# Summing two halves of a norm product ahead of a matmul with ones, and taking the norm's inverse root on ScalarE

## The chip, the cores and the metric

The kernel runs on one core of a Trainium2 chip. Times are device microseconds of that core; a run's time is compared by the median of several executions. A separate execution, taken by the hardware profiler, gives the profile.

## What is computed

Two cross-attention layers follow each other on x (16 batches, 256 query tokens, 320 channels, 20 heads of 16), with a context of 256 tokens of 512 channels per batch. The change touches the second layer only. Cut to what matters, with 252 text tokens and 4 image tokens:

```python
probs_t = softmax(q @ k_t.T * scale)                 # per head, 256 x 252
text_out = probs_t @ v_t
qsem = probs_t @ text_ehs                            # per head, 256 x 512
qsem = qsem / max(norm(qsem), 1e-12)
ip_n = ip_ehs / max(norm(ip_ehs), 1e-12)
fused = q @ k_ip.T * scale + 0.5 * (qsem @ ip_n.T)
probs_ip = softmax(fused) * spatial_mask
out = (text_out + probs_ip @ v_ip) @ W_out + b_out + residual
```

The long vectors qsem are never formed. Their squared norm is p' G p, where p is a row of probabilities and G the 252 x 252 matrix of products of the text tokens (the Gram matrix).

## The kernel before

Work is cut into slots: a slot is one group of four heads of one batch, five slots to a batch, 80 slots for the first layer and 80 for the second. `slot1(k)` writes out the order of TensorE's work in a slot of the second layer by hand; between its parts `fill` steps through background tasks (projections, keys, values, the image softmax, the output of the batch before), each of which has a list of due times. Only TensorE's order is pinned in the slots. The order on VectorE (DVE in the profile), ScalarE (ACT), GpSimd (POOL) and the DMA-issuing SyncE (SP) is made by a scheduler, from the order in which operations are recorded and its own picture of their times.

A slot k of the second layer goes like this:

- `both1(k, t)`, for the two halves t of the text keys: transposed scores for slot k in the two PSUM banks "T" (L775), scores for slot k + 2 in "S" (L780) with their row maxima on VectorE (L781, tile `mn`), and the exponential on ScalarE (L786) into P, which has a tile for each of the two pairs of heads u, [128, 2 halves, 2 heads, 256].
- `rounded1(k, u)`: ScalarE writes a rounded half of P into R (L804, tile `ctb`), and GpSimd the rest P - R into W (L805, tile `wt`), each a 128x512 operation per half t.
- `norm1(k, u, n)`, one slot later: for each half n of the keys, four or three matmuls multiply the Gram blocks `gm` with R (L814), and VectorE multiplies the result by W, in place (L815). Each result takes one of the three PSUM banks "X", which rotate among these products, the background's matmuls and the transposed maxima (L792).
- `attend1(k)`, two slots later, at the start of a slot: eight matmuls gather the values (L823), and eight more with the matrix `zone` (L826), whose one column of ones adds W up over the keys of both halves n, into the same PSUM tile "P".
- `settle1` transposes the tile (L870), and divides (L873, L874). The norm goes into `nt`, column 5.

After a batch's last group, `image_softmax` works on all five groups at once, 128x40 values: u = max(norm, a tiny multiple of the squared row sum) (L889 on GpSimd, L891 on VectorE), then its inverse root r as the power -1/2 on GpSimd (L894), the fused scores a (L897, L899), their maximum m4 (L902), the exponential (L906), its sum and the reciprocal (L909, L910), and the products with the mask (L912, L914). VectorE transposes the outcome (L921), `close1` multiplies it with the image values (L931), adds it to the gathered heads (L932), splits the sum into two parts (`split`, tile `ho`: L511 on ScalarE, L512 and L513 on VectorE) and projects it (L522). `image1` (L500) and the projection of the next query tokens (`hq`) are other background work that the prediction speaks of. In the last batch the image softmax runs twice, for four groups and for the last one.

The power's exponent is a tile of -0.5, `w1["mhalf"]`, which `weights3` puts into a corner of a buffer.

Of the kernel before, what the change touches and what calls it, by code (L numbers as in the profile page):

```python
# [10 lines left out]
AF = mybir.ActivationFunctionType  # L11
ALU = mybir.AluOpType
# [4 lines left out]
B = 16  # L17
S = 256
# [3 lines left out]
CP = 384  # L22
# [8 lines left out]
NG = H // 4  # L31
# [10 lines left out]
def RAMP(t):  # L42
    return t if t < -5 or t > 3 else (t + 5) * 0.375
# [5 lines left out]
def xattn2(  # L49
# [27 lines left out]
    nc = tc.nc  # L77
    f = lambda ap: ap.bitcast(F32)
    mm = nc.tensor.matmul

    def dma(out, in_):
        nc.sync.dma_start(*(f(ap) if ap.dtype == FR else ap for ap in (out, in_)))
# [6 lines left out]
    def bank(tag="X"):  # L89
        return ps.tile([128, 512], F32, tag=tag, name=tag, bufs=BANKS[tag])  # L90
# [8 lines left out]
    def buf(tag, shape, dtype=F32, bufs=1, name=None):  # L99
        if tag in ("wB", "wD", "vr", "raw"):  # L100
            return sb.tile(shape, dtype, tag=tag, name=name or tag, bufs=bufs)
        size = 1
        for d in shape[1:]:
            size *= d
        if tag not in slots:
            slots[tag] = [0, dtype] + [const_tile([128, max(size, words.get(tag, 0))], f"{tag}_{i}", dtype) for i in range(bufs)]
        n, kind, *ring = slots[tag]
        assert kind == dtype and len(ring) == bufs, tag
        slots[tag][0] += 1
        t = ring[n % bufs][: shape[0], :size]  # L110
        names = "abcd"[: len(shape) - 1]
        if len(names) > 1:
            t = t.rearrange(f"p ({' '.join(names)}) -> p {' '.join(names)}", **dict(zip(names, shape[1:])))
        return t

    def const_tile(shape, tag, dtype=F32):
        return const.tile(shape, dtype, tag=tag, name=tag)
# [162 lines left out]
    zone = const_tile([128, 32], "zone")  # L280
# [82 lines left out]
    w1, v1t, gmt = {}, [], []  # L363
# [70 lines left out]
    def weights3():  # L434
        gm = buf("vr", [128, 3 * (H * V0W + 16)], FR, bufs=3, name="gm")
        gm = gm[:, : 7 * 128].rearrange("p (g n) -> p g n", n=128)
        nc.gpsimd.memset(f(gm), 0.0)
        gmt.append(gm)
        yield
        if len(gmt) == 2:  # L440
            one, two = [buf("rs", [128, 2 * S], bufs=2, name="one") for i in range(2)]
            w1["vb"], w1["mhalf"] = one[:, :CP], one[:, CP : CP + NG * 8]
            w1["pT"], w1["pip"] = two[:, :S], two[:, S:].rearrange("p (f c) -> p f c", c=32)
            nc.vector.memset(w1["mhalf"], -0.5)
            nc.gpsimd.memset(w1["pip"], 0.0)

    ct1 = {}
# [158 lines left out]
    QK, P, W, R = {}, {}, {}, {}  # L606
# [202 lines left out]
    def norm1(k, u, n):  # L809

        gm = get("t1", k // NG - B)[1]
        yp = bank().rearrange("p (h t) -> p h t", h=2)
        for i, (gb, kt) in enumerate(blocks[n]):
            mm(yp, gm[:, gb], R[k, u][:, kt], start=i == 0, stop=i == len(blocks[n]) - 1)  # L814
        nc.vector.tensor_mul(W[k, u][:, n], yp, W[k, u][:, n])  # L815

    def attend1(k):
        b, g = divmod(k - NS, NG)
        v, pv = get("t1", b)[0], bank("P")
        for n in range(2):  # L820
            for s in range(4):
                h = V1W * (4 * g + s)
                mm(pv[32 * s : 32 * s + 32, :S], v[:, n, h : h + 32], P[k, s % 2][:, n, s // 2], start=n == 0, stop=False)  # L823
        for n in range(2):
            for s in range(4):
                mm(pv[32 * s : 32 * s + 32, :S], zone, W[k, s % 2][:, n, s // 2], start=False, stop=n == 1)  # L826
        settle1(b, g, pv)

    def slot1(k):
# [30 lines left out]
    def settle1(b, g, pv):  # L860
        hn = hsn
        if g == 0:
            norms[b] = buf("tmp", [128, NG, 8, 6], bufs=2, name="n1")
        nt = norms[b]
        if "na" not in w1:
            w1["na"], masks = [buf("nt", [128, 2, 8, 32], bufs=2, name="na") for i in range(2)]
            w1["bmask"] = masks.rearrange("p a f c -> p (a f c)")[:, :CP]
            dma(w1["bmask"], bmask_d)
        na = w1["na"][:, (NG * b + g) % 2]
        nc.vector.transpose(na.rearrange("p f c -> p (f c)"), pv[:, :S])  # L870
        nc.gpsimd.tensor_copy(nt[:, g], na[:, :, 16:22])
        rz = pv[:, S : S + 8]
        nc.vector.reciprocal(rz, na[:, :, 16])  # L873
        nc.vector.tensor_mul(  # L874
            hn[:, g // 2, :, g % 2], na[:, :, 0:16], rz.unsqueeze(2).to_broadcast([128, 8, 16])
        )
        if g == NG - 1:
            nc.gpsimd.tensor_copy(hn[:, 2, :, 1], hn[:, 2, :, 0])
            later(0.4, lambda: gather(1, b))

    def image_softmax(b, lo=0, hi=NG):

        gs, n = slice(lo, hi), hi - lo
        nt, si = norms[b][:, gs], get("o1", b)[1]
        pool = nc.gpsimd
        small = lambda n, t: buf(t, [128, NG, 8] + ([n] if n > 1 else []))[:, gs]

        u = small(1, "u")
        pool.tensor_mul(u, nt[:, :, :, 0], nt[:, :, :, 0])  # L889
        yield  # L890
        nc.vector.scalar_tensor_tensor(u, u, EPS2 / 4, nt[:, :, :, 5], op0=ALU.mult, op1=ALU.max)  # L891
        yield
        r = small(1, "r")
        pool.tensor_tensor(r, u, w1["mhalf"].rearrange("p (f s) -> p f s", f=NG)[:, gs], op=ALU.pow)  # L894
        b4 = lambda t: t.unsqueeze(3).to_broadcast([128, n, 8, NIP])
        a = small(NIP, "a")
        pool.tensor_mul(a, nt[:, :, :, 1:5], b4(r))  # L897
        by_group = lambda t: t[:, :, : NG * NIP].rearrange("p f (g n) -> p g f n", n=NIP)[:, gs]
        pool.tensor_add(a, a, by_group(si))  # L899
        yield  # L900
        m4 = small(1, "m4")
        nc.vector.tensor_reduce(m4, a, axis=AX.X, op=ALU.max)  # L902
        yield
        pool.tensor_sub(a, a, b4(m4))
        yield
        nc.scalar.activation(a, a, AF.Exp, scale=SCALE)  # L906
        yield
        z4 = small(1, "z4")
        nc.vector.tensor_reduce(z4, a, axis=AX.X, op=ALU.add)  # L909
        nc.vector.reciprocal(z4, z4)  # L910
        yield
        pool.tensor_mul(z4, z4, mk.unsqueeze(1).to_broadcast([128, n, 8]))  # L912
        pi = w1["pip"]
        pool.tensor_mul(by_group(pi), a, b4(z4))  # L914
        if hi < NG:
            return
        vb = w1["vb"]
        dma(vb, vipd[NIP * b : NIP * (b + 1)].unsqueeze(0).to_broadcast([32, NIP, CP]))
        yield
        pT = w1["pT"]  # L920
        nc.vector.transpose(pT, pi.rearrange("p f c -> p (f c)"))  # L921
        nc.vector.tensor_mul(vb, vb, w1["bmask"])
        return pT, vb
# [38 lines left out]
    def task(key, times, make, *needs):  # L962
        tasks[key] = [times, 0, make, needs, len(tasks)]
# [14 lines left out]
    def get(*key):  # L978
        while key not in results:
            step(key)  # L980
        return results[key]
# [20 lines left out]
    def shifted(n, *times):  # L1002

        return [RAMP(n + t) for t in times]
# [10 lines left out]
    for c in range(B // 2):  # L1015
        n, k = 10 * c, [("k0", c)] if c else []
# [11 lines left out]
    for b in range(B):  # L1028
        n = NS + 5 * b
        task(("k1", b), shifted(n, -7, -6.67, -6.33, -5.67, -5, -4.67), lambda b=b: keys1(b), ("w2",), *([("t1", b - 1)] if b else []), *([("w4", 1)] if b > 2 else []))  # L1030
        task(("t1", b), shifted(n, -3.67, -3, -2.67, -2.33), lambda b=b: tokens1(b), ("k1", b), ("w3", b % 2))
        task(("o1", b), shifted(n, -7.67, -7, -6.67, -5.33, -4.33, -4), lambda b=b: open1(b), ("w7",), ("c0", b), *([("o1", b - 1)] if b else []))
        task(("i1", b), shifted(n, 6.67, 6.67, 6.67, 7.33, 7.33, 7.67, 7.67, 8, 8.33), lambda b=b: image_softmax(b, NG - 1 if b == B - 1 else 0), ("gathered", 1, b), ("taken", B + b - 1), *([("i1a",)] if b == B - 1 else []))
        task(("c1", b), shifted(n + (1.67 if b > B - 3 else 0), 8.67, 8.67, 8.67, 8.67, 9, 9.67, 11.67, 13), lambda b=b: close1(b), ("i1", b), ("w4", 1))
    task(("i1a",), [2 * NS + 0.1], lambda: image_softmax(B - 1, 0, NG - 1), ("i1", B - 2))
    spread = lambda t, d, n: [t + d * i for i in range(n)]
    thirds = lambda n, t: [t + i // 3 + (0.2, 0.6, 1.0)[i % 3] for i in range(n)]
# [4 lines left out]
    for i in range(2):  # L1042
        task(("w3", i), [NS - 4 + 5 * i], weights3)
# [147 lines left out]
```

## Time and profile before

| | |
|---|---|
| median of 3 runs | 1643.64 us (1639.58 to 1647.11) |
| profiled execution, time | 1646.73 us |
| profiled execution, span from the first to the last instruction | 1644.9 us |
| busy: TensorE, its weight load | 94%, 75% |
| busy: VectorE, ScalarE, GpSimd | 73%, 50%, 72% |
| mean granted TensorE clock | 0.972 |
| second layer, one batch | about 55.1 us |

Busy shares are averages over the whole span; the two layers differ, so a stage is read by itself. A line such as L815 is a line of the kernel before. In a group's row stand the line, the engine, the operation, what it writes and reads, sizes, and the number of instructions; then the busy time in us and the mean of one in ns; then the idle time of that engine just ahead of them, and what ended it. A matmul of full-width floats appears as two records.

### The profile page before, as it was taken

The page shows a single profiled execution, that of the slowest core. Times are in us where ns is not written, and L with a number is a line of the kernel's source. Part 1 is how long each engine was busy: PE and PEld are TensorE (multiplying, and loading weights), DVE is VectorE, ACT ScalarE, POOL GpSimd, SP SyncE. Part 2 cuts the span into 40 slices and gives each one's busy share as a digit, 9 for nine tenths or more (in the row PEclk, how much of TensorE's full clock was granted, in tenths as well). Part 3 has the DMA queues.
Part 4 walks back from the last instruction along what each step waited for, and adds up shares of the span by engine and source line. Part 5 has one row for each costly group of instructions (what it writes and reads, how often), then busy time and mean ns, then how long its engine had stood idle before and what let it go on. Part 6 is the DMA issues. An engine that isn't in the chain of part 4 may idle for free.

```text
span 1644.9 us, 36268 instructions
## 1 busy us (share of the span) xinstructions
PE 1539.0 (94%) x13306; PEld 1239.6 (75%) x13306; DVE 1197.1 (73%) x2404; ACT 830.3 (50%) x1797; POOL 1184.0 (72%) x1131
## 2 busy tenths in 40 slices
PE   7789999999999899689999999999999999999996
PEld 6677878787878787577777777777777777777765
DVE  5467777677666677867777787778777887787685
ACT  5335445445454545435555455545555555555462
POOL 3358787868686867767687767767776787678675
PEclk9799999999999999789999999999999999999998
DMA  7766777777777676565324333343334233423301
GB/s 220 203 207 197 219 202 218 202 210 196 207 198 222 180 213 172 162 198 179 121 86 132 119 104 108 124 127 97 115 118 133 88 123 110 142 82 106 109 26 44
DMA packets 247742, 247.49 MB, mean 150 GB/s; under 512 B 31050, under 2 KB 231468, under 8 KB 247564
## 3 DMA queue, kind: packets, MB, share of 16 engines
q1 hardware_dynamic: 245356, 243.87, 50.1%
q8 instruction: 106, 1.74, 0.5%
q10 hardware_dynamic: 2208, 1.30, 0.3%
q14 instruction: 72, 0.59, 0.1%
HBM read 121.21 MB, written 88.18 MB: 127 GB/s over the span
## 4 chain that ended last, share of the span: by engine, by line
PE 54%; DVE 14%; DMA 10%; POOL 9%; ACT 5%; issue 4%; SPq 2%; ACTq 0%; POOLq 0%; DVEq 0%
PE X L205 16%; PE X L814 10%; PE X L522 7%; PE P L709 5%; POOL wt L805 4%; PE S L649 3%; PE P L823 3%; PE T L673 3%; DMA qs<-qd 3%; PE P L826 3%; PE T L775 2%; DMA qs<-mt 2%; DVE ho L512 2%; DMA kd<-kst 2%; DVE wt L815 2%
## 5 line engine op out<-in xcount | busy, mean ns | idle before, releaser
L679 POOL TENSOR_TENSOR P<-P,rs 128x512 f32<-128x512 f32 x320 | 412.6, 1310 | 171.3 <-ACT P L676 170.9
L805 POOL TENSOR_TENSOR wt<-P,ctb 128x512 f32<-128x512 f32 x320 | 422.4, 1335 | 117.1 <-ACT ctb L804 115.9
L814 PE MATMUL X<-ctb,gm 128*128 128x512 f32 x1120 | 328.8, 412 | 2.5 <-DVE wt L815 2.5
L676 ACT ACTIVATE P<-T 128x512 f32<-128x512 f32 x320 | 176.2, 595 | 234.5 <-PE T L673 118.4
L786 ACT ACTIVATE P<-T 128x512 f32<-128x512 f32 x320 | 174.1, 597 | 142.4 <-PE T L775 121.8
L815 DVE TENSOR_TENSOR wt<-X,wt 128x512 f32<-128x512 f32 x320 | 216.7, 679 | 25.7 <-PE X L814 23.0
L804 ACT ACTIVATE ctb<-P 128x512 fp32r<-128x512 f32 x320 | 195.8, 631 | 74.9 <-PE X L814 63.2
L814 PEld LDWEIGHTS X<-ctb,gm 128*128 128x128 f32 x1120 | 188.8, 188 | 49.4 <-DVE wt L815 5.2
L781 DVE TENSOR_REDUCE mn<-S 128x4 fp32r<-128x1008 f32 x160 | 191.1, 1194 | 0.6 <-PE S L780 0.6
L651 DVE TENSOR_REDUCE mn<-S 128x4 fp32r<-128x716 f32 x160 | 142.6, 891 | 0.0
L673 PE MATMUL T<-qs,ks 127*128 127x256 f32 x640 | 112.6, 296 | 22.9 <-DVE tmp L726 9.8
L649 PE MATMUL S<-ks,qs 125*128 125x256 f32 x640 | 119.1, 310 | 11.2 <-DVE mn L651 3.5
L709 PE MATMUL P<-P,vr 128*32 128x256 f32 x1920 | 128.9, 404 | 0.0
L649 PEld LDWEIGHTS S<-ks,qs 125*128 125x128 f32 x640 | 89.9, 197 | 48.3 <-issue 38.3
L522 PE MATMUL X<-ho,wF 128*128 128x256 f32 x768 | 112.9, 290 | 7.1 <-DVE ho L512 3.0
L894 POOL TENSOR_TENSOR r<-u,rs 128x40 f32<-128x40 f32 (+2 forms) x17 | 108.7, 6393 | 14.8 <-DVE u L891 14.7
L522 PE MATMUL X<-hq,wE 128*128 128x256 f32 x768 | 110.7, 288 | 6.6 <-POOL hq L512 3.1
L673 PEld LDWEIGHTS T<-qs,ks 127*128 127x128 f32 x640 | 93.3, 199 | 28.0 <-DVE tmp L726 11.7
L522 PEld LDWEIGHTS X<-ho,wF 128*128 128x128 f32 x768 | 103.6, 195 | 12.8 <-DVE ho L512 4.7
L522 PEld LDWEIGHTS X<-hq,wE 128*128 128x128 f32 x768 | 102.9, 194 | 11.0 <-POOL hq L512 3.8
L205 PE MATMUL X<-cta,wA 128*128 128x252 f32 (+1 forms) x720 | 100.9, 287 | 7.7 <-ACT wA L147 5.8
L650 DVE TENSOR_REDUCE mn<-S 128x4 fp32r<-128x308 f32 x160 | 74.8, 468 | 44.8 <-PE S L649 44.2
(196 smaller groups left out, 2814.9 us busy)
## 6 DMA issues: line engine op xcount, KB each, us to landing
qd<-q SPq DMA_DIRECT2D x96, 384.0 KB
qs<-tph SPq DMA_DIRECT2D x64, 308.0 KB
kd<-kst SPq DMA_DIRECT2D x73, 256.0 KB
rawc<-in_cT_dram SPq DMA_DIRECT2D x60, 256.0 KB
qs<-qd SPq DMA_DIRECT2D x80, 192.0 KB
ks<-kd SPq DMA_DIRECT2D x80, 192.0 KB
ks<-kd SPq DMA_DIRECT2D x160, 96.0 KB
qs<-qd SPq DMA_DIRECT2D x160, 96.0 KB
```

Of the source, the lines that this page charges most:

```text
L205: last = mm(out, lhs(a, k), rhs(b, k), start=i == 0, stop=i == len(terms) - 1)
L522: mm(pp, w(s, k, slice(m * 128, (m + 1) * 128)), a[:, t], start=i == 0, stop=i == len(terms) - 1)
L649: mm(sp[:, h], Q[: XROW + T0, h, t * 128 : (t + 1) * 128], K[: XROW + T0, h], start=True, stop=True)
L673: mm(st[p][:, j], K[:KS0, 2 * p + j, t * 128 : (t + 1) * 128], Q[:KS0, 2 * p + j], start=True, stop=True)
L676: exp = anchor(nc.scalar.activation(pt, st[p], AF.Exp, scale=SCALE))
L679: anchor(nc.gpsimd.tensor_mul(pt, pt, rs[:, t : t + 1].to_broadcast([128, 2, S])))
L709: mm(pv[32 * s : 32 * s + 32, o : o + S], v[:, vt, h : h + 32], P[k, s // 2][:, t, s % 2], start=vt < 2, stop=vt != 1,)
L781: anchor(nc.vector.tensor_reduce(maxes[k + 2][:, t], sp[:, :, :T1], axis=AX.X, op=ALU.max))
L804: nc.scalar.activation(R[k, u][:, t], P[k, u][:, t], AF.Copy, scale=0.5)
L805: anchor(nc.gpsimd.tensor_sub(W[k, u][:, t], P[k, u][:, t], f(R[k, u][:, t])))
L814: mm(yp, gm[:, gb], R[k, u][:, kt], start=i == 0, stop=i == len(blocks[n]) - 1)
L815: nc.vector.tensor_mul(W[k, u][:, n], yp, W[k, u][:, n])
```

## The change

Per slot, the two halves of the product W are added elementwise before they meet the ones, so that four products with `zone` are left of eight; the sum runs on GpSimd for the first pair of heads and on VectorE for the second. In the image softmax the inverse root is taken as exp(-1/2 ln(2^20 u) + 10 ln 2) by two ScalarE activations, in a step of its own with the same due time; the tile of exponents becomes one column holding 10 ln 2.

```diff
-            w1["vb"], w1["mhalf"] = one[:, :CP], one[:, CP : CP + NG * 8]
+            w1["vb"], w1["shift"] = one[:, :CP], one[:, CP : CP + 1]
...
-            nc.vector.memset(w1["mhalf"], -0.5)
+            nc.vector.memset(w1["shift"], 6.931471805599453)
...
-        nc.vector.tensor_mul(W[k, u][:, n], yp, W[k, u][:, n])
+        w = W[k, u]
+        nc.vector.tensor_mul(w[:, n], yp, w[:, n])
+        if n:
+            (nc.vector if u else nc.gpsimd).tensor_add(w[:, 0], w[:, 0], w[:, 1])
...
-        for n in range(2):
-            for s in range(4):
-                mm(pv[32 * s : 32 * s + 32, :S], zone, W[k, s % 2][:, n, s // 2], start=False, stop=n == 1)
+        for s in range(4):
+            mm(pv[32 * s : 32 * s + 32, :S], zone, W[k, s % 2][:, 0, s // 2], start=False, stop=True)
...
-        pool.tensor_tensor(r, u, w1["mhalf"].rearrange("p (f s) -> p f s", f=NG)[:, gs], op=ALU.pow)
+
+        nc.scalar.activation(r, u, AF.Ln, scale=2.0**20)
+        nc.scalar.activation(r, r, AF.Exp, bias=w1["shift"], scale=-0.5)
+        yield
...
-        task(("i1", b), shifted(n, 6.67, 6.67, 6.67, 7.33, 7.33, 7.67, 7.67, 8, 8.33), ...
+        task(("i1", b), shifted(n, 6.67, 6.67, 6.67, 6.67, 7.33, 7.33, 7.67, 7.67, 8, 8.33), ...
```

More of the change, by code (lines that the diff above doesn't have):

```diff
@@ L1032, in xattn2 @@
         task(("o1", b), shifted(n, -7.67, -7, -6.67, -5.33, -4.33, -4), lambda b=b: open1(b), ("w7",), ("c0", b), *([("o1", b - 1)] if b else []))
-        task(("i1", b), shifted(n, 6.67, 6.67, 6.67, 7.33, 7.33, 7.67, 7.67, 8, 8.33), lambda b=b: image_softmax(b, NG - 1 if b == B - 1 else 0), ("gathered", 1, b), ("taken", B + b - 1), *([("i1a",)] if b == B - 1 else []))
+        task(("i1", b), shifted(n, 6.67, 6.67, 6.67, 6.67, 7.33, 7.33, 7.67, 7.67, 8, 8.33), lambda b=b: image_softmax(b, NG - 1 if b == B - 1 else 0), ("gathered", 1, b), ("taken", B + b - 1), *([("i1a",)] if b == B - 1 else []))
         task(("c1", b), shifted(n + (1.67 if b > B - 3 else 0), 8.67, 8.67, 8.67, 8.67, 9, 9.67, 11.67, 13), lambda b=b: close1(b), ("i1", b), ("w4", 1))
```

## The prediction

> **What bounds the kernel now.** I began with the page: busy times first, then its costliest groups for the lines that the change touches.
>
> ```profile
> PE 1539.0 (94%) x13306; PEld 1239.6 (75%) x13306; DVE 1197.1 (73%) x2404; ACT 830.3 (50%) x1797; POOL 1184.0 (72%) x1131
> ...
> L805 POOL TENSOR_TENSOR wt<-P,ctb 128x512 f32<-128x512 f32 x320 | 422.4, 1335 | 117.1 <-ACT ctb L804 115.9
> L815 DVE TENSOR_TENSOR wt<-X,wt 128x512 f32<-128x512 f32 x320 | 216.7, 679 | 25.7 <-PE X L814 23.0
> ...
> L894 POOL TENSOR_TENSOR r<-u,rs 128x40 f32<-128x40 f32 (+2 forms) x17 | 108.7, 6393 | 14.8 <-DVE u L891 14.7
> ```
>
> TensorE is the fullest engine. The change lies wholly in the second layer (from about 780 us), where one batch of five slots repeats every 55.1 us. So I cut one batch, slot by slot, with the table of busy time by stage (span; then PE, PEld, DVE, ACT, POOL, granted clock, DMA).
>
> ```profile
> 1196.50:1206.90 10.40, 10.40 (x95) 8.07 (x95) 8.83 (x15) 5.41 (x11) 5.57 (x7) 1.00 0.49 161
> 1206.90:1218.30 11.40, 11.40 (x100) 9.04 (x96) 7.52 (x13) 5.58 (x11) 9.49 (x7) 1.00 0.67 202
> 1218.30:1229.20 10.90, 10.90 (x102) 8.52 (x98) 8.69 (x20) 6.40 (x15) 10.13 (x12) 1.00 0.00 0
> 1229.20:1238.60 9.40, 9.40 (x84) 6.79 (x80) 7.71 (x15) 6.62 (x13) 8.01 (x9) 1.00 0.56 177
> 1238.60:1251.60 13.00, 12.22 (x108) 9.45 (x104) 10.17 (x17) 5.96 (x14) 7.74 (x8) 1.00 0.17 54
> ```
>
> Call these slots A to E. TensorE stands still only in E, for 0.78 us; VectorE has 42.9 of 55.1 us. The chain of waits for the seam of D and E says who makes TensorE late there:
>
> ```profile
> 1230.75 0.48 POOL rs L914
> ...
> 1231.26 0.04 DVE rs L921
> ...
> 1236.23 1.00 DVE hT L932 x3
> ...
> 1237.25 0.84 ACT ho L511
> ...
> 1238.12 1.57 DVE ho L512
> 1239.69 1.43 DVE ho L513
> ...
> 1243.49 0.59 DVE wt L815
> ```
>
> From 1231 to 1244 the chain is nearly all VectorE; elsewhere in the batch it is TensorE. So TensorE's saving counts in slots E, A, B and C, and VectorE's load counts in the stretch D to E. Last, the timeline of slot B, where the norm's root is taken:
>
> ```profile
> 1209.68 0.22 DVE L891 SCALAR_TENSOR_TENSOR u<-u,tmp 128x40 f32<-128x40 f32 x1
> ...
> 1209.98 6.77 POOL L894 TENSOR_TENSOR r<-u,rs 128x40 f32<-128x40 f32 x1 [0.98 <-DVE u L891]
> ...
> 1211.90 1.21 DVE L781 TENSOR_REDUCE mn<-S 128x4 fp32r<-128x1008 f32 x1
> ...
> 1213.03 0.68 DVE L815 TENSOR_TENSOR wt<-X,wt 128x512 f32<-128x512 f32 x1
> ...
> 1214.47 0.28 PE L792 MATMUL X<-ident_r,mn 128*4 128x128 f32 x2
> ```
>
> **The change, part by part, for one batch.**
>
> *Removed from TensorE.* The chain gives the eight products with the ones (L826) 0.86 us, so four cost 0.43 us: 80 x 0.43 = 34.4 us in all, 2.15 per batch. Four of the five savings (1.72 us) lie where TensorE leads; slot D's falls beside the VectorE stretch and is worth nothing.
>
> *Removed from GpSimd.* 17 powers, 108.7 us. They are not on TensorE's path by themselves, but they push the image softmax late: VectorE waits for L914 before L921, 14.9 us over 12 batches, 1.24 each. In the changed program's order L921 stands a slot earlier. VectorE then enters the stretch unhurried: L815 begins when TensorE ends its three matmuls (about 1236.6) and not behind L932 at 1237.14, 0.47 us earlier counting a handover of 0.08 (L891's end to L894's start), and the 0.30 us that L512 waited for ScalarE is room too: 0.77 us.
>
> *Added on GpSimd.* 80 sums of 128x512 at 1.31 us (its 128x512 rows: 1.28 to 1.34) are 105 us, so GpSimd's total stays. They stand between the two subtractions of a slot's first pair. Those results are wanted a slot later, so I cost this at nothing; the cover is gone if GpSimd is over a slot behind.
>
> *Added on VectorE.* 80 sums of 128x512, both operands in SBUF. Alone such a sum takes 0.67 to 0.69 us (L148 wB, cta). While GpSimd works it is slower: L512 ho, same shape, median 1.57; L513 ho, half the size, 1.51, and 0.47 where it comes before GpSimd starts. So one costs a = 0.67 to 1.57. At the end of every slot GpSimd works on its last two L805, so the sum mostly meets a running one; L500's shape runs at a median of 1.22 against 0.55 alone (L148 wA), in between. I take a = 1.1. The Trainium skill ("SBUF — State Buffer", "SBUF: two separate sides") says that such an operation and a GpSimd one exclude each other for the whole instruction. By that alone the worst a would be 1.33 + 0.69 = 2.0, an estimate, against the row's 1.57; it speaks against putting this sum on VectorE.
>
> Where does the sum end late? In D and E it stands in the chain, ahead of L512: a. In the other slots it must be done before TensorE reaches the ones, about 2.2 to 2.8 us after its last L814. Behind it are queued L500 (A), L870 and L781, which free the banks:
> - E: L815 ends 1248.74, ones at 1250.64: free.
> - A: L815 ends 1204.63, ones at 1205.88. At a = 1.1 TensorE, 0.4 early by then, waits 0.2, and the two L500, L870, L781 and L815 slip by 0.3 behind it: 0.5 (0 to 0.9).
> - C: the sum stands behind L486 and L490, which ended at 1228.16; ScalarE's casts for them now come some 0.6 earlier, so it ends 1228.3 to 1229.1, the ones were due at 1228.21: 0.5 (0 to 0.9).
>
> *Root on ScalarE.* In the built program each of the 17 softmax passes has two table loads, one before the logarithm, one before the exponential. The three loads in this trace take 1.28 us, and the activation starts 0.01 after L676's. ScalarE gains about 17 x (2 x 1.28 + 0.5) = 52 us and has room (30.0 of 55.1 us busy). The first load needs nothing and hides before u. What hurts stands on VectorE: the changed order puts the maximum L902 right behind slot B's first two L815, ahead of L781. It needs Ln (0.25, near L376's 0.20), load 1.28, Exp 0.3 (near L906's 0.23), L897 0.48, L899 0.53 and handovers: 3.1 us after u's 1209.90, so 1213.0. VectorE would be there at 1211.92: it waits 1.1 (0.3 if its own L500 have slipped by 0.8, 1.6 if GpSimd first ends half an L805), does L902 in 0.3, and L781 and the next L815 come 1.4 late. L792 takes the bank that this L815 frees (three banks in turn): freed at 1215.1 for 1213.7, wanted at 1214.47. That leaves 0.65 beyond the slack, and TensorE, 0.4 early, loses that too: 1.1 (0.2 to 1.6). Queued behind the logarithm on ScalarE are L469, L804, the next two L786 and the DMAs of L796; they come 1.2 late and hide: the L786's banks are wanted again at 1218.3, L796's rows a slot later.
>
> Two rules of the skill ("ScalarE: Activation LUTs") would move this. "Table sets: the hidden batching unit" says one set holds both functions, so Ln then Exp needs one load; with none in the chain slot B's wait would be gone and the sum by it near -7 us. "What ACT_TABLE_LOAD costs" gives 2.66 us for a switch, drain included, 1.38 more in the chain: by it some +32 us. The built order and the 1.28 rows go between.
>
> *Sum.* Per batch, net = a + s - (1.72 + 0.77), s being the waits in A, B and C: 1.1 + (0.5 + 1.1 + 0.5) - 2.49 = +0.7 us; 16 batches, +11. In the tail the last powers (5.44 and 1.65 us, alone on the chain ahead of the last L931) become two pairs of about 3 us, the first partly hidden: -1. So +10. The profiled execution took 1646.7 us (span 1644.9, 1.8 around it): 1656.7 on that basis. It lies 3.1 above the median of 1643.6, so I forecast 1654.
>
> **Rivals.**
> - *VectorE's waits eat the saving* (forecast): slower by over 0.5%, which is about what a measurement of this kernel can tell from no change (8 us). a from 1.1 to 1.57 with s 2.1 to 3: +0.7 to +2.1 per batch, 1654 to 1676; the case begins at a + s = 3.0, 1652. For it: the 1.51 to 1.57 rows, and the place of L902. Against: VectorE has 12 us of each batch free.
> - *TensorE stays the bound* (faster). Place: the new VectorE sum, and L902 in slot B. It decides from a + s under 2.0 per batch: a sum at 0.7, before GpSimd's next L805, and L902's wait under the 0.76 us that L792's bank had spare. At a = 0.7, s = 0.6 net is -1.2, 16 x -1.2 = -19: 1624. If all is hidden and the stretch gives way too, -34: 1609. For it: TensorE is busy in 54.3 of 55.1 us, and VectorE's 1.24 us wait for L914 goes.
> - *Even*: a + s between 2.0 and 3.0, 1636 to 1652: the same mechanism with smaller stalls.
> - *ScalarE's chain is longer than the rows say*, by one load's length: L902's wait 2.4, +1.3 x 16 on the forecast: 1675.
>
> **How the numbers follow.** Waits eat the saving 0.48, ScalarE's longer chain 0.06, even 0.2, TensorE's saving 0.26. So faster 0.26, same 0.2, slower 0.54. Both signs hold much: the forecast's own range is 1652 to 1676. The range for 8 in 10 runs from -17 us (1627, the faster case without its best part) to +34 (1678, a = 1.57 and s = 3).
>
> **What would show it.** Right: L826's successor at half the records; the new VectorE sums near 1.1 us; L902 waiting about 1 us for GpSimd each batch; new TensorE waits before L792 and before the ones, about 2 us per batch; two loads of 1.28 us per batch; no L921 wait. Wrong: sums at 0.7, no TensorE wait for them, and a batch near 54 us; or batches beyond 57.5 us.

## The result, and the profile after

The changed kernel takes **1664.64 us** (median of 4 runs, 1663.67 to 1669.91), against 1645.38 us for the kernel before in the same comparison (4 runs, 1639.58 to 1647.60): a ratio of **1.0123 [1.0089, 1.0157]**, some 20 us slower. The profiled executions say the same: 1665.17 us with a span of 1663.4, against 1646.73 and 1644.9, so +18.5 us in the span.

Lines move by a few in the changed kernel: the product is L816, the sum L818, the products with the ones L828, u L893, Ln L897, Exp L898, the maximum L907, the image sum on VectorE L926. L781 (row maxima) and L792 keep theirs.

First the page of the changed kernel: its totals and its groups for the product, the sums and GpSimd's weighting (busy us, mean ns of one | idle before).

```profile
PE 1533.5 (92%) x12666; PEld 1222.9 (74%) x12666; DVE 1317.2 (79%) x2484; ACT 877.7 (53%) x1865; POOL 1202.2 (72%) x1194
...
L805 POOL TENSOR_TENSOR wt<-P,ctb 128x512 f32<-128x512 f32 x320 | 451.0, 1424 | 76.0 <-ACT ctb L804 75.6
...
L818 POOL TENSOR_TENSOR wt<-wt 128x512 f32<-128x512 f32 x80 | 103.3, 1292 | 14.8 <-DVE wt L816 14.7
...
L818 DVE TENSOR_TENSOR wt<-wt 128x512 f32<-128x512 f32 x80 | 106.1, 1326 | 2.1
```

TensorE lost 640 records of matmuls (320 products of two records each) but only 5.5 us of busy time, in a longer span; VectorE gained 120 us, of which its 80 sums are 106. Those take 1.33 us in the mean; the product L816, of the same shape but with one operand in PSUM, takes 0.68. GpSimd's L805 went from 1335 to 1424 ns beside them. One sum with its neighbours on GpSimd, from the timeline (start, us):

```profile
1246.06 1.29 POOL L148 TENSOR_TENSOR cta<-rawc,cta 128x512 fp32r<-128x512 f32 x1
...
1246.59 1.31 DVE L818 TENSOR_TENSOR wt<-wt 128x512 f32<-128x512 f32 x1
...
1247.31 3.43 POOL L805 TENSOR_TENSOR wt<-P,ctb 128x512 f32<-128x512 f32 x2
```

The sum ends 0.55 us after GpSimd's operation that was running when it began, and the L805 that starts meanwhile takes longer: the two here 3.43 us together. Of the 80 sums, 75 began beside such a 128x512 operation; all 75 ended 0.545 to 0.553 us after its end. Three that met an idle GpSimd took 0.68 to 0.69.

Next the waits of the changed kernel from 860 to 1600 us, some 13 batches (us in total, times, longest us).

```profile
DVE m L907 <- POOL a L904: 19.9, 13, 1.6
...
PE P L828 <- DVE wt L818: 9.5, 14, 0.9
...
PE X L792 <- DVE mn L781: 8.5, 12, 1.0
...
PE S L780 <- DVE mn L781: 6.3, 14, 0.8
...
DVE rs L926 <- POOL rs L919: 4.6, 13, 0.4
...
PE X L814 <- DVE wt L816: 2.5, 13, 0.2
...
PEld P L828 <- DVE wt L818: 29.2, 52, 1.3
```

Two of the four waits of TensorE's matmuls are new: for VectorE's sum ahead of the ones, 9.5 us, and for the row maxima ahead of L792, 8.5. The other two were there before, as long (6.5 and 2.3 us in the same window). VectorE's wait for GpSimd before the image sum (14.9 before) has shrunk to 4.6, and a wait for the maximum, 1.5 us per batch, stands in its place.

The 9.5 us are not all that TensorE loses to the sum: the last line counts 29.2 us of its weight loads' waits. The timeline shows the products with the ones of one slot. Before, in slot C:

```profile
1228.21 1.05 PE L826 MATMUL P<-wt,zone 128*32 128x256 f32 x16
```

And after, in slots B and D:

```profile
1226.63 1.03 PE L828 MATMUL P<-wt,zone 128*32 128x256 f32 x8
...
1246.69 0.59 PE L828 MATMUL P<-wt,zone 128*32 128x256 f32 x2
...
1247.95 0.63 PE L828 MATMUL P<-wt,zone 128*32 128x256 f32 x6 [0.67 <-DVE wt L818]
```

From the first start to the last end, the eight took 1.05 us in every slot. The four take 0.61 in slot E alone; in A, B, C and D they take 1.27, 1.05, 0.97 and 1.89 (means of nine batches), because the second pair's sum comes late. Over a batch that is 5.8 us, against 5.2 for the eight: what the four products save is lost at the same place.

Where the second wait of TensorE comes from shows in the timeline of slot B of one batch (start, us, engine, line, [idle before it, and for whom]).

```profile
1218.95 0.23 DVE L893 SCALAR_TENSOR_TENSOR u<-u,tmp 128x40 f32<-128x40 f32 x1
...
1219.20 0.24 ACT L897 ACTIVATE r<-u 128x40 f32<-128x40 f32 x1 [1.03 <-DVE u L893]
...
1219.46 1.28 ACT L898 ACT_TABLE_LOAD   x1
...
1220.76 0.33 ACT L898 ACTIVATE r<-r,rs 128x40 f32<-128x40 f32 x1
...
1222.28 0.32 DVE L907 TENSOR_REDUCE m<-a 128x40 f32<-128x160 f32 x1 [1.58 <-POOL a L904]
...
1222.52 1.20 DVE L781 TENSOR_REDUCE mn<-S 128x4 fp32r<-128x1008 f32 x1
...
1222.87 0.22 PE L792 MATMUL X<-ident_r,mn 128*4 128x128 f32 x1
...
1223.77 0.22 PE L792 MATMUL X<-ident_r,mn 128*4 128x128 f32 x1 [0.69 <-DVE mn L781]
```

From the end of u (1218.95 + 0.23 = 1219.18) to the maximum L907 pass 3.10 us, 1.28 of them the table load between the two activations. VectorE stands idle for 1.58 of these; the row maxima L781, queued behind L907, come late by that, and the second L792 has to wait 0.69 us for them.

Last the chain of waits of the changed kernel from that slot to the next batch.

```profile
1226.81 0.84 PE P L828 x8
...
1246.59 1.31 DVE wt L818
1247.90 1.69 DVE ho L512
1249.59 1.44 DVE ho L513
...
1252.11 1.16 DVE mn L781
...
1253.39 0.59 DVE wt L816
...
1260.39 0.43 PE P L828 x8
```

The four products with the ones hold the chain for 0.43 us where the sum is done in time (the last line), and for 0.84, as long as the eight did, where they wait for it. At the seam of D and E the sum lies on the chain with its full 1.31 us, and L512 behind it with 1.69 (1.76 from its own start; 1.57 before).

The batch, u to u, takes 56.13 us in the mean of ten, against 55.17: +0.96. The span splits up by the u's like this: layer one -2.3 us, the second layer up to its first u +5.1, the middle 12 batches +11.5, the next three intervals together +5.3, and from there to the end -1.1: +18.5.

### The profile page after: what moved, and what is told of

Same layout as the page of the kernel before. It is cut to its first block, busy times and chain, and to the rows that moved or that the text cites. A ratio compares the mean times of both kernels' runs of the same rounds, so it can differ in the third digit from the quotient of the medians.

```text
span 1663.4 us, 35253 instructions
## 1 busy us (share of the span) xinstructions
PE 1533.5 (92%) x12666; PEld 1222.9 (74%) x12666; DVE 1317.2 (79%) x2484; ACT 877.7 (53%) x1865; POOL 1202.2 (72%) x1194
## 4 chain that ended last, share of the span: by engine, by line
PE 55%; DVE 18%; DMA 10%; POOL 4%; SPq 4%; issue 3%; ACT 3%; ACTq 0%; DVEq 0%; POOLq 0%
PE X L205 14%; PE X L814 12%; PE X L522 8%; PE P L709 5%; DMA qs<-qd 4%; SPq L82 4%; PE S L649 3%; DVE mn L781 3%; DVE wt L818 3%; PE T L673 3%; PE P L826 3%; PE T L775 2%; DVE wt L816 2%; PE P L828 2%; DVE ho L512 2%
## 5 line engine op out<-in xcount | busy, mean ns | idle before, releaser
L805 POOL TENSOR_TENSOR wt<-P,ctb 128x512 f32<-128x512 f32 x320 | 451.0, 1424 | 76.0 <-ACT ctb L804 75.6
L816 DVE TENSOR_TENSOR wt<-X,wt 128x512 f32<-128x512 f32 x320 | 215.3, 678 | 17.4 <-PE X L814 16.9
L804 ACT ACTIVATE ctb<-P 128x512 fp32r<-128x512 f32 x320 | 195.3, 632 | 61.5 <-PE X L814 60.8
L781 DVE TENSOR_REDUCE mn<-S 128x4 fp32r<-128x1008 f32 x160 | 191.1, 1194 | 0.6 <-PE S L780 0.6
L522 PE MATMUL X<-ho,wF 128*128 128x256 f32 x768 | 112.4, 289 | 6.7 <-DVE ho L512 2.9
L522 PE MATMUL X<-hq,wE 128*128 128x256 f32 x768 | 111.9, 289 | 5.8 <-ACT hq L511 3.1
L818 POOL TENSOR_TENSOR wt<-wt 128x512 f32<-128x512 f32 x80 | 103.3, 1292 | 14.8 <-DVE wt L816 14.7
L522 PEld LDWEIGHTS X<-ho,wF 128*128 128x128 f32 x768 | 103.0, 194 | 12.5 <-DVE ho L512 4.6
L522 PEld LDWEIGHTS X<-hq,wE 128*128 128x128 f32 x768 | 102.7, 194 | 11.4 <-POOL hq L512 5.2
L818 DVE TENSOR_TENSOR wt<-wt 128x512 f32<-128x512 f32 x80 | 106.1, 1326 | 2.1
```

The lines of the kernel that those rows point to most:

```text
L522: mm(pp, w(s, k, slice(m * 128, (m + 1) * 128)), a[:, t], start=i == 0, stop=i == len(terms) - 1)
L781: anchor(nc.vector.tensor_reduce(maxes[k + 2][:, t], sp[:, :, :T1], axis=AX.X, op=ALU.max))
L804: nc.scalar.activation(R[k, u][:, t], P[k, u][:, t], AF.Copy, scale=0.5)
L805: anchor(nc.gpsimd.tensor_sub(W[k, u][:, t], P[k, u][:, t], f(R[k, u][:, t])))
L816: nc.vector.tensor_mul(w[:, n], yp, w[:, n])
L818: (nc.vector if u else nc.gpsimd).tensor_add(w[:, 0], w[:, 0], w[:, 1])
```

## The experiments

Each ratio is against the kernel before, run beside it on the same chip over five rounds, with its 95% interval; us worked out from ratios take 1645 us as 1. A difference of two such ratios is good to some 4 to 7 us. Where "the batch" is given, it is u to u in the run's one profile, the mean of ten.

**e1_sum_only: the sums without the new root.** The kernel before with the sums and four products; the power stays on GpSimd.

```diff
-        nc.vector.tensor_mul(W[k, u][:, n], yp, W[k, u][:, n])
+        w = W[k, u]
+        nc.vector.tensor_mul(w[:, n], yp, w[:, n])
+        if n:
+            (nc.vector if u else nc.gpsimd).tensor_add(w[:, 0], w[:, 0], w[:, 1])
...
-        for n in range(2):
-            for s in range(4):
-                mm(..., zone, W[k, s % 2][:, n, s // 2], start=False, stop=n == 1)
+        for s in range(4):
+            mm(..., zone, W[k, s % 2][:, 0, s // 2], start=False, stop=True)
```

> The sums and the four products with the ones are as in the changed kernel; the root stays the power on GpSimd. VectorE theory (the sum, slowed by GpSimd at the shared port, and the maximum m4 waiting for the root): the sum costs 1.33 us in the D to E stretch and about 0.5 each in A and C, less 1.72 saved, so +0.6 us per batch, 1650 to 1660, and no wait for m4; the wait before L921 of 1.2 us comes back. ScalarE theory (the root's table loads are the whole loss): TensorE's saving comes through, 1612 to 1630. GpSimd theory (its late subtractions are the loss): GpSimd now has the powers and the sums, so 1665 or more, with TensorE or VectorE waiting for L805.

1731.49 us, 1.0537 [1.0515, 1.0559]: 88 us slower, far beyond what my theory allowed. The chain of waits of this kernel shows where it begins:

```profile
1250.54 6.77 POOL r L896
1257.31 1.23 POOL wt L805
1258.54 1.23 POOL wt L818
...
1259.81 1.08 PE P L828 x8
```

GpSimd's sum stands in its queue behind the power, and TensorE cannot reach the ones before it: 28.8 us of TensorE waits on GpSimd's sum (12 times, up to 2.6 us) between 860 and 1600 us. From about the end of each of the twelve the granted TensorE clock is 0.5 for 3.4 or 6.8 us, 65 us in all (it is 1.00 from 860 to 1600 us in the kernel before and in the changed one); the four products above fall into such a stretch and take 1.08 us. Half speed over 65 us would cost some 32 us, an estimate, as much as the waits themselves. Before the change nothing that a slot's own ones needed came that late from GpSimd. So the two halves of the change belong together: the sum on GpSimd is cheap only because the power has left it. VectorE's sums, though, do not wait for the power: the 16 that ran beside it took 0.68 to 0.69 us.

**e2_root_only: the new root without the sums.** The change's root, its added step and due time, eight products.

```diff
-        pool.tensor_tensor(r, u, w1["mhalf"]..., op=ALU.pow)
+        nc.scalar.activation(r, u, AF.Ln, scale=2.0**20)
+        nc.scalar.activation(r, r, AF.Exp, bias=w1["shift"], scale=-0.5)
+        yield
```

> The root is the logarithm and exponential on ScalarE; the eight products with the ones stay and nothing is summed ahead. VectorE theory: m4 still stands ahead of L781 and waits about 1.1 to 1.6 us for the root, which costs TensorE about 1 us in slot B, against 0.8 us gained where the power's delay goes: -5 to +10 us, 1640 to 1655. ScalarE theory: +20, about 1665. GpSimd theory: GpSimd loses 7 us per batch, so faster than before, 1620 to 1635.

1642.62 us, 0.9993 [0.9979, 1.0006]: no change. GpSimd's busy time falls from 1184 to 1076 us, the maximum waits 1.0 us per batch (13.8 us, 14 times), but TensorE waits for L781 ahead of L792 only once, 0.4 us, so that wait reaches nobody else. Taken together, the 109 us of powers off GpSimd and the table loads come to nothing as long as no sums are there. That each is worth nothing by itself is not shown: no run has the one without the other. TensorE's waits at least hardly move (10.2 us in the window, 8.8 before), although VectorE waits longer ahead of the image sum, 32.0 us (14.9 before).

**e3_m4_behind: the maximum queued later.** The changed kernel with L907 made to follow the next product on VectorE, so that slot B's row maxima go ahead of it; the due time of one step is moved from 7.33 to 6.67 to fit.

```diff
-        nc.vector.tensor_mul(w[:, n], yp, w[:, n])
+        muls[:] = [nc.vector.tensor_mul(w[:, n], yp, w[:, n])]
...
-        nc.vector.tensor_reduce(m4, a, axis=AX.X, op=ALU.max)
+        queued(nc.vector.tensor_reduce(m4, a, axis=AX.X, op=ALU.max), *muls)
```

> The changed kernel with one edit: the maximum m4 is queued on VectorE behind slot B's L781 and the product after it. VectorE theory: the 1.6 us wait goes, and with it TensorE's wait before L792 (about 1.1 to 1.5 us per batch): 1642 to 1650, the sum's part of the loss staying. ScalarE theory: ScalarE's work is unchanged and so is the time, 1660 to 1668. GpSimd theory: unchanged too.

1680.76 us, 1.0224 [1.0202, 1.0247]: slower still, where I expected a gain. The L907 wait is gone, but VectorE now waits 24.6 us (13 times, up to 2.1) at the next step of the same softmax, for ScalarE's exponential, and 16.5 us before the image sum. The softmax is a serial chain: with one step pushed back and its successors not, VectorE meets the wait one step on.

**e4_psum_sum: the same sum with one operand in PSUM.** For VectorE's pair the second half's product is left in its PSUM bank, and the sum reads that bank and the first half.

```diff
+        if n and u:
+            nc.vector.tensor_mul(yp, yp, w[:, n])
+            nc.vector.tensor_add(w[:, 0], yp, w[:, 0])
+            return
...
-            (nc.vector if u else nc.gpsimd).tensor_add(w[:, 0], w[:, 0], w[:, 1])
+            nc.gpsimd.tensor_add(w[:, 0], w[:, 0], w[:, 1])
```

> The changed kernel with one edit: for the pair of heads whose sum runs on VectorE, the second half's product stays in its PSUM bank, so that the sum reads one operand from PSUM and one from SBUF. VectorE theory: the sum takes 0.68 us in place of 1.33 and does not wait for GpSimd, L512 goes back from 1.76 towards 1.57, the waits before the ones shrink; -1.2 to -1.6 us per batch: 1640 to 1648. ScalarE theory: no change, 1660 to 1668. GpSimd theory: L805 goes back from 1424 to 1335 ns, 7 us per core less, with a smaller gain, 1655 to 1662.

1653.15 us, 1.0063 [1.0039, 1.0088]: about 10 us, half of the loss, comes back (the batch is 55.35 us, against 56.13). In the groups of this kernel from 860 to 1600 us:

```profile
L818 DVE TENSOR_TENSOR wt<-X,wt 128x512 f32<-128x512 f32 x68 | 46.8, 689 | 1.9
...
L931 DVE TENSOR_TENSOR rs<-rs,nt 128x384 f32<-128x384 f32 x13 | 20.3, 1559 | 0.0
...
L512 DVE TENSOR_TENSOR ho<-hT,ho 128x512 fp32r<-128x512 f32 x13 | 9.2, 709 | 0.0
```

The sum takes 0.69 us instead of 1.33, beside the same work of GpSimd, and L512 behind it 0.71 instead of 1.76; L805 is back at 1338 ns. L512's gain is lost again two instructions on, at the multiplication of the image values with a mask (L931 here, L927 in the changed kernel, also with both operands in SBUF): 1.56 us, against 0.55. L512, L513 and this multiplication take 3.77 us together, against 3.74, so what comes back in this stretch is the sum's part alone. TensorE's wait for VectorE's sum falls from 9.5 to 0.5 us. But a wait that the changed kernel did not have shows up, ahead of L522 in slot C, for VectorE's L490 of the Gram block: 18.7 us, 13 times.

**e5_no_loads: the changed kernel without table loads.** Exp stands in the place of Ln, so the root is left out, and the two activations need no load.

```diff
-        nc.scalar.activation(r, u, AF.Ln, scale=2.0**20)
+        nc.scalar.activation(r, u, AF.Exp, scale=2.0**-20)
```

> The changed kernel with an exponential in place of the logarithm (the norm's root is left out, its two instructions stay), so that ScalarE loads no table in the second layer; the order on every engine is that of the changed kernel. Theory that m4's wait is the second load in the chain: L907's wait falls from 1.58 us to about 0.3, TensorE's wait before L792 goes, 0.8 to 1.3 us per batch: 1644 to 1652. Rival, that VectorE's load alone sets the time and the wait is only slack used up: 1660 to 1666.

1653.03 us, 1.0047 [1.0030, 1.0065]: about 12 us come back (the batch is 54.90 us). The wait for the maximum falls from 19.9 to 3.7 us, and TensorE's for L781 ahead of L792 is gone; the waits for the sum (10.5 us) stay, and the sum takes 1361 ns. So the loads are what makes the maximum late; that it is the second one, between the two activations, follows from the timeline above and not from a run. Without the sums they left TensorE a single wait of 0.4 us ahead of L792 (e2).

**e6_half_sum: only GpSimd's pair summed.** VectorE's sum is left out and its pair keeps four products: six in all.

```diff
-        if n:
-            (nc.vector if u else nc.gpsimd).tensor_add(w[:, 0], w[:, 0], w[:, 1])
+        if n and not u:
+            nc.gpsimd.tensor_add(w[:, 0], w[:, 0], w[:, 1])
...
-        for s in range(4):
-            mm(..., zone, W[k, s % 2][:, 0, s // 2], start=False, stop=True)
+        for s in (0, 2, 1, 3):
+            for n in range(1 + s % 2):
+                mm(..., zone, W[k, s % 2][:, n, s // 2], start=False, stop=n == s % 2)
```

> The changed kernel without VectorE's sums: GpSimd adds the halves of the first pair of heads as before, the second pair's two halves meet the ones as two products each, six products per slot. Theory that VectorE's sum is the loss: 1.33 us per slot leave VectorE, TensorE gets back two of four products (0.22 us per slot); against the kernel with the root alone (1642.6) TensorE saves 80 x 0.22 = 17 us: 1625 to 1640. Rival, that GpSimd's sums and the slowed subtractions cost as much as VectorE's: 1650 to 1665.

1650.34 us, 1.0017 [1.0003, 1.0032]: within half a per cent of before, not the gain I expected. Its chain of waits has

```profile
1206.05 0.88 PE P L829 x12
```

(each product shows as two records, so x12 is six): six products take as long as eight, and there is no saving to pay for anything. The loads and a wait for the maximum of 16.2 us are still there, and no wait of TensorE ahead of L792: the loads cost something only together with VectorE's sums and the four products.

**e7_half_late: e6 with the softmax where it stood before.** The steps from the maximum on are due a third of a slot later, with the maximum queued as in e3, which puts it behind slot C's row maxima.

```diff
-        task(("i1", b), shifted(n, 6.67, 6.67, 6.67, 6.67, 7.33, 7.33, 7.67, 7.67, 8, 8.33), ...
+        task(("i1", b), shifted(n, 6.67, 6.67, 6.67, 6.67, 7.67, 7.67, 8, 8, 8.33, 8.67), ...
```

> The kernel of e6 with m4 queued behind slot C's second L781 and the product after it, and the later steps of the image softmax due a third of a slot later, where the kernel before had them. If m4's wait costs TensorE what it did in the changed kernel (about 1 us per batch) and nothing new takes its place, 10 to 16 us under e6. If the wait only moves to L914 and L926 behind it, as with m4 behind slot B's L781, equal to e6 or up to 10 us slower.

1650.23 us, 1.0030 [1.0014, 1.0046]. No wait of VectorE for the maximum is left, and the time is that of e6: the wait was holding up nothing there.

**e8_late: the same for the changed kernel.** Its edit is e7's, made on the changed kernel.

> The changed kernel with the same queueing in slot C, its sums as they are. If m4's wait is worth 1 us per batch: 1645 to 1652. If the wait turns up again at L916 and L928: 1660 to 1680, as with m4 behind slot B's L781 (1680.8). VectorE's sums stay in both cases, so not below 1640.

1663.42 us, 1.0104 [1.0083, 1.0125]: no gain that the intervals show. The waits for the maximum and ahead of L792 are gone, but the softmax's work on VectorE is back in the stretch from C to E, and TensorE's wait for the sum grows to 12.3 us (27 times), the sum to 1407 ns. The batch is half a microsecond shorter (55.58 against 56.13), but the stretch up to the first u and the last batches are longer. With e3 this suggests that the maximum's wait and the crowded stretch are two places for the same load; no run shows it.

**e9_four_no_sum: the saving by itself.** The kernel before with the first half's four products alone. The second half's part of the norm is left out.

```diff
-        for n in range(2):
-            for s in range(4):
-                mm(..., zone, W[k, s % 2][:, n, s // 2], start=False, stop=n == 1)
+        for s in range(4):
+            mm(..., zone, W[k, s % 2][:, 0, s // 2], start=False, stop=True)
```

> The kernel before with one edit: only the first half of the keys meets the ones, four products per slot (the second half's part of the norm is left out), no sums, the root as a power on GpSimd. It shows TensorE's saving without any price. If the prediction's count is right (0.43 us in four of five slots, the fifth beside VectorE's stretch): -1.7 us per batch, 1612 to 1620. If TensorE is the bound all through: -34, 1609 to 1611. If VectorE's stretch sets most of a batch: 1630 or more.

1622.74 us, 0.9861 [0.9836, 0.9886]: halving these products brings 23 us here with no sum to pay for, not 34. The batch takes 53.36 us, 1.81 less. The ones stand on the chain with

```profile
1207.44 0.43 PE P L825 x8
```

and part of the rest is taken by TensorE's wait for L781 ahead of L780, 12.9 us against 6.5 before.

**e10_psum_no_loads: e4's edit and e5's together.** As in e5 the root is left out.

```diff
+            nc.vector.tensor_mul(yp, yp, w[:, n])
+            nc.vector.tensor_add(w[:, 0], yp, w[:, 0])
...
-        nc.scalar.activation(r, u, AF.Ln, scale=2.0**20)
+        nc.scalar.activation(r, u, AF.Exp, scale=2.0**-20)
```

> The changed kernel with both edits at once: the VectorE sum from PSUM, and an exponential in place of the logarithm (the root is left out), so that no table is loaded. Each alone gave 1653 of 1664.6. If the two losses are separate and add: 1639 to 1644, about the time of the kernel before. If they are one loss with two doors (VectorE's backlog in slot B): 1648 to 1654.

1643.62 us, 0.9990 [0.9972, 1.0007]: in the whole time the two losses add up (9.9 and 12.5 us by the ratios, 21.9 together), and without them the time is that of before. In the repeating batch they overlap: e4 takes 0.78 us off it, e5 1.23, both together 1.35 (54.78). So once the loads are gone, most of what the PSUM operand still brings lies in the first and last batches. But it is not e9's: 21 us of the possible saving are still missing. TensorE's largest wait is the one ahead of L522 for L490, 18.7 us.

**e11_six_in_turn: e6 in another order.** All four products of the first half, then the two of the second.

```diff
-        for s in (0, 2, 1, 3):
-            for n in range(1 + s % 2):
+        for n in range(2):
+            for s in range(4) if n == 0 else (1, 3):
```

> The kernel of e6 with its six products in another order: the four column groups of the first half in turn, then the two groups of the second half (e6 had the two halves of a group one after the other). If products of four column groups run side by side, so that only whole rounds of four cost time: 0.86 to 0.88 us on the chain as with eight or e6's six, and 1647 to 1653. If e6's order was what cost: 0.65 us, and 1633 to 1642.

1651.48 us, 1.0033 [1.0016, 1.0050]; the six take 0.86 us on the chain. The order does not matter. Each product fills one of four column groups, and 4 take 0.43 us, 6 and 8 take 0.86 to 0.88. That is what one expects if the four groups run side by side and the one with the most products, two in e6 and e11, sets the time. Taking two products from only two groups saves nothing.

**e12_psum_gm_first: e4 with the Gram block's steps ahead.** ScalarE's casts and VectorE's L486 and L490 of the Gram block (`gms` and `gmd` hold the last of each) are queued ahead of the second pair's L804 and ahead of the last product, so that the bank which L522 takes is read out earlier.

```diff
-            nc.scalar.activation(R[k, u][:, t], P[k, u][:, t], AF.Copy, scale=0.5)
+            half = nc.scalar.activation(R[k, u][:, t], P[k, u][:, t], AF.Copy, scale=0.5)
+            if u and gms:
+                queued(half, *gms)
...
-            nc.vector.tensor_mul(yp, yp, w[:, n])
+            prod = nc.vector.tensor_mul(yp, yp, w[:, n])
+            if gmd:
+                queued(prod, *gmd)
```

> The kernel of e4 with slot C's Gram block brought forward: its two casts stand ahead of the second pair's L804 on ScalarE, and VectorE's L486 and L490 ahead of the second pair's last product, so that the bank which the next L522 takes comes free earlier. If TensorE's wait of 1.4 us per batch for L490 is a loss of its own: 12 to 20 us under e4, 1632 to 1641, faster than the kernel before. If VectorE's load takes it back behind: 1648 to 1654.

1649.50 us, 1.0027 [1.0010, 1.0045], against e4's 1.0063 [1.0039, 1.0088]. The L522 wait went from 18.7 to 12.7 us, and the ratios differ by 5.9 us; the intervals overlap. The batch falls from 55.35 to 54.90, by 0.45, and the wait by 0.46 per batch. This points to that wait as a cause of what is missing; with one profile each it does not quite show it. No version that computes the whole reference beat the kernel before; e2 equals it.

## Why the prediction was right, and where its steps were off

Slower was right, by the mechanism it gave: the sums and the wait for the maximum on VectorE cost more than TensorE saves. The forecast rise was 10 us, the measured one 18.5 in the span. The sign was held with 0.54 only, and +0.7 per batch was what remained of costs of 3.2 and gains of 2.5, each with errors of that size: some luck is in it. Step by step:

- **TensorE's saving.** 0.43 us per slot and 1.72 per batch: e9 shows 0.43 and 1.81. That four of five slots count was right in size, though not by the chain as the text read it: from 1222 to 1231 us that chain is ScalarE and GpSimd, not TensorE. Sixteen such batches would be 29 us, and e9 gained 23; its profile has 21.1 us less in the middle 12 batches and only 2.2 in the last ones, where TensorE once waits 3.5 us for u, and the granted clock is 0.5 for 6.8 us around that wait's end. What the text did not see is that taking away fewer than one product per column group saves nothing (e6, e11).
- **VectorE's sum.** a = 1.1 was taken, 1.33 measured, inside 0.67 to 1.57 in the mean; single sums reached 1.83. The cause, both operands in SBUF while GpSimd works on a 128x512 operation, is shown by e4 and by the 75 sums that end 0.55 us after that operation. The exclusive lock of the Trainium skill ("SBUF — State Buffer", "SBUF: two separate sides") agrees: the sum waits for the rest of the running operation, the next L805 for the sum, and the sum with a PSUM operand, which the page's rule leaves out, ran at 0.69. The estimate of 2.0 by that rule is the case of a sum that meets an operation just begun; the longest was 1.83, and the mean depends on when the sum begins.
- **Where the sum ends late.** E was free, as forecast. In A and C the four products with the ones take 0.66 and 0.36 us longer than the 0.61 they need, for 0.5 and 0.5. B was left out, and costs 0.44 (0.03 in e5, so it comes with the loads); D, taken as the sum's place on the chain, costs 1.28.
- **What the sum does behind itself.** L512 was thought to gain 0.47 + 0.30 us of room (the 0.77 in the forecast's sum). Its wait for L511, 0.3 per batch, is gone. But it got slower, from a median of 1.57 to 1.76, as it begins when GpSimd's operation has more of its time left, and L805 went from 1335 to 1424 ns; the prediction had no term for either.
- **GpSimd's sums at nothing.** True in this change but for one wait of 0.8 us in the last batch, and for a reason the text did not give: with the power still on GpSimd the sums make the kernel 88 us slower (e1).
- **The root.** The chain of 3.1 us was exact; VectorE's wait came to 1.58 in the batch shown and 1.53 in the mean, for 1.1, inside its bounds of 0.3 to 1.6. The step after it named the wrong resource: TensorE's second L792 waits for its data, the row maxima, and not for the bank that L816 frees; the first L792 ran at 1222.87, before that L816 began at 1223.63. TensorE's wait there is 0.7 us, for 1.1. The loads' price is 12 us (e5). The rule by which one load would serve both functions ("ScalarE: Activation LUTs", "Table sets: the hidden batching unit") does not show here: the trace has two loads of 1.28 us per pass. The drain of "What ACT_TABLE_LOAD costs" does not show either: the load starts 0.02 us after Ln's end and Exp 0.02 after the load's.
- **The powers taken off GpSimd.** 1.24 us per batch of L921's wait were to give 0.77 with the room for L512. The wait did shrink, to 0.35, but no run shows that this is worth anything: in e2 the powers are gone and the time is that of before. If the 0.77 was not there, the costs of the middle batch were 0.96 + 1.81 = 2.8 and not the 3.2 forecast, and two misses offset each other.
- **The sum.** +0.7 per batch forecast, +0.96 measured: 3 of the 8.5 us by which the forecast fell short. The step that failed most is the multiplication by 16: the stretch up to the first u and the last batches, counted like the middle ones at some 3 us in all, cost 10.4. Up to the first u VectorE is busy for 45.5 of 51.6 us (37.3 of 46.5 before), and there TensorE waits for VectorE's sum up to 2.8 us at a time, against 0.9 in the middle. The tail gave -1.1, as forecast. Layer one was 2.3 us shorter, which the change does not touch.
- **The rivals.** A TensorE bound with the sums hidden fell with a = 1.33 and the products above. "ScalarE's chain longer by a load" fell: the chain was 3.10. "Even" is what e10 reaches, with neither the slow sum nor the load.

**The account, and what stays open.** The change is some 43 us above e9's 0.9861, the saving with no price. e4 and e5 show 10 of these for the sum's two SBUF operands and 12 for the loads, each good to some 6 or 7 us. The other 21 are not split up by any run. The traces say where TensorE loses them in the batch, which is 1.42 us longer in e10 than in e9: the four products at the seam of D and E take 1.27 us instead of 0.61, and the wait for L490 is 1.4, while the wait ahead of L780 is some 0.5 shorter than in e9. e12 points to the L490 wait; that VectorE is simply 0.69 us per slot fuller may be the same thing seen from the other side.

## What to carry to other kernels

An engine with a quarter of its time free had no free place here for one more instruction: find out where in its queue the instruction stands, what its neighbours' operands are, and who waits for what is queued behind it. An elementwise sum on VectorE was better fed from PSUM here, where GpSimd works beside it; look also for the instruction that inherits the wait (L931 in e4). Look for a late operand in the consumer's own duration too: four products that wait between one another show as busy time. And cost the first and last iterations of a pipelined loop from their own stretches of the trace, not as copies of the middle one.

## What the runs showed of the hardware that was not expected

- Products into four column groups: 4 take 0.43 us, 6 take 0.86 to 0.88, 8 take 0.86, in either order (e6, e9, e11).
- The VectorE sum of 128x512 costs 1.33 us in the mean with two SBUF operands, 0.69 with one in PSUM. It is a wait, not a slower pace: it ends 0.55 us after GpSimd's running 128x512 operation (0.545 to 0.553 in 75 sums), and the L805 that starts meanwhile takes 1.73 us on average instead of 1.29. So L512 (also two SBUF operands) takes 1.76 us in the changed kernel and 0.71 in e4, where it begins 0.15 us before GpSimd's operation ends.
- GpSimd's power of 128x40 (6.77 us) holds up no such sum: 16 beside it took 0.68 to 0.69 us (e1).
- From about the end of each of twelve TensorE waits of 1.8 to 2.6 us in e1, the granted clock was 0.5 for 3.4 or 6.8 us.
- A switch of activation tables took 1.28 us with 0.02 us on either side; logarithm and exponential, one after the other, needed two.
